# Attention in 128-query chunks: scores kept in SBUF pages, maxima sent through DRAM

## The chip, the cores and the metric

The kernel runs on one core of one Trainium2 chip. The metric is the device time of one execution in microseconds (us); the time before is 3614.04 us, the median of three runs (3613.12 to 3618.05). Engines are named as the profile names them: PE is TensorE, DVE is VectorE, ACT is ScalarE, POOL is GpSimd, and SP issues nearly all DMAs.

## The reference, cut to what matters

The kernel computes one transformer block on x of 8 batches, 1024 tokens and 512 channels, in f32. A condition gives shifts, scales and gates.

```
mod = silu(condition) @ Wada + bada                       # 6 parts: sh_a, sc_a, gt_a, sh_m, sc_m, gt_m
xm = layernorm(x, g1, be1) * (1 + sc_a) + sh_a
q, k, v = heads(xm @ Wqkv)                                # 16 heads of 32 channels
scores = q @ k.T * 32 ** -0.5                             # causal mask: -inf above the diagonal
x = x + gt_a * (softmax(scores) @ v @ Wproj + bproj)
xm = layernorm(x, g2, be2) * (1 + sc_m) + sh_m
x = x + gt_m * (gelu(xm @ W1 + b1) @ W2 + b2)
```

The softmax subtracts each query's maximum. Only the attention between q, k, v and the projection `Wproj` changes here.

## The kernel before, in words

The work is cut into 16 blocks of 512 tokens (`blocks`): an even block is the first half of a batch and attends to itself alone, an odd block is the second half and attends to both halves. A block has four groups of four heads (128 channels, `NC` = 4, `HPG` = 4); a head's 32 channels fill one quarter of PE's rows, so the four heads' score matmuls run side by side.

**The linear work** (q, k, v, the two layers of the MLP) is written as Strassen products: `matmul` at L201 issues four matmuls of 128 rows by 32 columns, weights come through a ring of nine 256 KB pieces (`RING`, `fetch`, L335 and L337 on SP). Results leave three PSUM banks (`banks`) on DVE or ACT (`copy_out`, `combine_out` at L193). An f32 matmul of the program shows as two instructions in the trace.

**Attention of one group** makes the scores twice. `scores_at_once` (L1389) puts queries on partitions and keys along the free dimension, 512 columns at a time for four heads, in the PSUM tile `st` (four banks, one buffer). DVE adds the causal mask on the diagonal (L1403) and reduces the maxima (L1406). `split_maxima` (L1420 to L1428) splits each maximum into three bf16 numbers, `maxima_rows` turns them into rows by bf16 matmuls (L1444), and ACT copies them out (L1450). `weights_T` then makes the scores again with keys on partitions (L1469), and bf16 matmuls subtract the maxima inside PSUM (L1481). ACT takes the exponential from PSUM into one of three `pT` tiles (L1493), POOL zeroes what lies above the diagonal (L1498), `weigh` multiplies by v (L1521), and `add_weights` sums the weights of all keys on POOL (L1594). `finish` sums them over partitions with a matmul by ones (L1539), ACT copies the sums and the result out (L1545, L1548), DVE inverts in four parts (L1554), and POOL multiplies (L1571).

**The order** is fixed when the kernel is built. A planner keeps a clock for each engine (`now`), notes each instruction's cost and when its results are due, and interleaves the attention units with the linear steps listed in `plan`: `step_aside` issues linear work while a unit is not ready, and `pace` spreads a window's linear work over its attention units. Each engine, and SP's queue, executes its list in that order and waits on semaphores.

Of the kernel before, what the change touches and what calls it, by code (L numbers as in the profile page):

```python
# [9 lines left out]
F32 = mybir.dt.float32  # L10
BF16 = mybir.dt.bfloat16
# [11 lines left out]
def kernel(  # L23
# [48 lines left out]
    RING = 9  # L72

# [153 lines left out]
    def mlp_steps(n):  # L227
# [7 lines left out]
        + [("mod", 3), ("at", 2), ("v", 1), ("mod", 4), ("columns_m",), ("k", 2), ("gates", "m")],  # L235
    }
    late = []
    for w in range(1, NB):
# [7 lines left out]
        if w == NB - 1:  # L246
            steps = late[:1] + [("load_xr", n)] + rows_a + [("proj", n), ("mt", n)] + late[1:]
            steps += [("v", w)] + rows_m + own + m[3:6]
            late = m[6:]
        else:  # L250

            steps = late + [("v", w), ("load_xr", n)] + rows_a + [("proj", n), ("k", w + 1)]
            if w == 1:
                steps = [("load_xr", n)] + rows_a + [("proj", n)]
            steps += [("mt", n), ("q", w + 1)] + rows_m + own
# [10 lines left out]
    plan[NB] = [("load_xr", n), late[0], ("beside", late[1]), ("proj", n), ("mt", n)] + mlp_steps(n)  # L266
# [120 lines left out]
    mask = const.tile([P, 2 * P], F32, tag="mask", name="mask")  # L387
    for i in range(2):
        make_causal_mask(nc, mask[:, ts(i, P)], MASKED)
# [4 lines left out]
    minus_ones = const.tile([P, P], BF16, tag="minus_ones", name="minus_ones")  # L394
    nc.gpsimd.memset(minus_ones, -1.0)
    mcols = const.tile([P, NTT, P], BF16, tag="mcols", name="mcols")
    nc.gpsimd.memset(mcols, 0.0)
    ident_b = const.tile([P, P], BF16, tag="ident_b", name="ident_b")
    nc.vector.tensor_copy(ident_b, ident)


    cond_act = tmp.tile([P, TB], F32, tag="top", name="cond_act", bufs=1)[:B, :]
# [41 lines left out]
    def norm_columns(name, shift_at, gain_at, o_g, o_b):  # L444
# [3 lines left out]
        one_plus = small.tile([P, NC, B], F32, tag="onep", name=f"onep{name}")  # L448
# [165 lines left out]
    def modulated(key, gain, shift, b, guards):  # L614
# [19 lines left out]
        for c in range(NC):  # L634
# [22 lines left out]
            if c == 1:  # L657
                nc.vector.tensor_tensor(part["T1"], part["T1"], part["B11"], ALU.subtract)
                note("DVE", 700, [at["B11"], at["T1"]], [at["T1"]], port=True)
        nc.vector.tensor_tensor(part["T2"], part["B22"], part["T1"], ALU.subtract)  # L660
# [14 lines left out]
    qTs, kTs, vs = {}, {}, {}  # L675
    projected, valued = set(), set()
# [163 lines left out]
    def project_T(step, store, pool, tag, done):  # L840

        n = step[1]
        dst = pool.tile([P, NC, TB], F32, tag=tag, name=f"{tag}_{n}")
        store[n] = dst
# [405 lines left out]
    def step_aside(reads, writes):  # L1250


        while threads():
            if linear_wait() == NEVER:
                hurry()
# [512 lines left out]
```

## Time and profile before

| What | Value |
|---|---|
| Median of three runs | 3614.04 us |
| Span of the profiled execution | 3610.1 us |
| The profiled execution's own time, taken as span plus the 3.9 us between span and median | 3614.0 us |
| PE, DVE, ACT, POOL busy | 98%, 58%, 37%, 56% of the span |
| Granted TensorE clock, mean | 0.995 |
| DMA engines' share | 38.8% on the main queue, 430.35 MB |

The profile shows one execution, which has no time of its own beside its span; the runs around it lie 3.0 to 8.0 us above that span. A line of a group reads: code line, engine, operation, output and inputs, shape, count, then busy time and the mean duration of one instruction. Busy time is the union of the group's intervals, so a mean duration holds the pipeline's latency too; the distance between two starts in the timeline is what a stretch of matmuls costs in a row.

### The profile page before, as it was taken

What the parts mean: (1) busy time and instruction counts of PE and PEld (TensorE: products, weight loads), DVE (VectorE), ACT (ScalarE), POOL (GpSimd) and SP (SyncE); (2) the same over time, 40 slices, a digit from 0 to 9 for tenths busy, and PEclk for the clock granted to TensorE, in tenths of its full rate; (3) what the DMA queues carried; (4) which work ended last, traced back from release to release, by engine and by line L of the source; (5) the groups of instructions that cost most, each with busy time, mean ns of one, the idle gap of its engine ahead of it and who ended that gap; (6) DMA issues with size and microseconds to landing.
All of it is one profiled execution on the core that took longest, in us unless ns stands there. A gap on an engine that the chain in (4) does not pass through costs nothing.

```text
span 3610.1 us, 121129 instructions
## 1 busy us (share of the span) xinstructions
PE 3537.6 (98%) x54821; PEld 1777.0 (49%) x54821; DVE 2078.8 (58%) x2316; ACT 1325.9 (37%) x1388; POOL 2038.3 (56%) x2187
## 2 busy tenths in 40 slices
PE   8999999999999999999999999999999999999999
PEld 5434445445554455544555455454554545545445
DVE  6765675563755547465464655746557455564663
ACT  2335334252433523335243351424524244232421
POOL 3666746665456753666536665456654566544660
PEclk9989999999999999999999999999999999999999
DMA  6633333434343343433434334343343433435334
GB/s 202 220 117 104 109 104 110 127 98 128 112 118 110 104 133 113 133 92 98 133 109 148 91 93 132 105 141 101 99 128 105 139 101 101 124 92 155 90 111 138
DMA packets 307894, 430.35 MB, mean 119 GB/s; under 512 B 25900, under 2 KB 176236, under 8 KB 307380
## 3 DMA queue, kind: packets, MB, share of 16 engines
q1 hardware_dynamic: 307264, 422.56, 38.8%
q8 instruction: 432, 7.08, 0.8%
q14 instruction: 82, 0.67, 0.1%
q10 hardware_dynamic: 116, 0.03, 0.0%
HBM read 394.12 MB, written 28.38 MB: 117 GB/s over the span
## 4 chain that ended last, share of the span: by engine, by line
PE 90%; DVE 4%; POOL 2%; ACT 2%; issue 1%; DMA 0%; SPq 0%; ACTq 0%; DVEq 0%; POOLq 0%
PE bank L201 62%; PE st L1469 8%; PE sc L1389 8%; PE po L1521 7%; DVE mx L1406 2%; PE st L1481 2%; PE bank L641 2%; PE bank L1539 2%; POOL pT L1594 1%; POOL xr L161 1%; ACT pT L1493 1%; DVE hT L1003 0%; PE bank L1444 0%; DVE xr L158 0%; ACT hT L945 0%
## 5 line engine op out<-in xcount | busy, mean ns | idle before, releaser
L1594 POOL TENSOR_TENSOR pT<-pT,pT 128x384 f32<-128x384 f32 (+2 forms) x1266 | 1195.6, 981 | 400.4 <-PE po L1521 211.0
L1493 ACT ACTIVATE pT<-st 128x2048 f32<-128x2048 f32 x288 | 541.0, 1878 | 858.2 <-PE st L1481 826.5
L201 PE MATMUL bank<-w,hT 128*32 128x256 f32 x14336 | 805.6, 381 | 1.0 <-ACT rec L1545 0.9
L1406 DVE TENSOR_REDUCE mx<-sc 128x4 f32<-128x2048 f32 (+3 forms) x380 | 658.5, 1754 | 147.7 <-PE sc L1389 140.6
L201 PEld LDWEIGHTS bank<-w,hT 128*32 128x32 f32 x14336 | 455.2, 110 | 338.4 <-issue 42.7
L201 PE MATMUL bank<-xm_m,w 128*32 128x256 f32 x8192 | 498.3, 381 | 3.1 <-ACT xm_m L651 3.0
L201 PE MATMUL bank<-t_m,w 128*32 128x256 f32 x6144 | 392.2, 381 | 0.4 <-DVE t_m L660 0.4
L1498 POOL TENSOR_SCALAR_AFFINE_SELECT pT<-pT 128x512 f32<-128x512 f32 x256 | 162.1, 651 | 400.4 <-ACT pT L1493 400.4
L201 PEld LDWEIGHTS bank<-xm_m,w 128*32 128x32 f32 x8192 | 254.9, 110 | 229.9 <-issue 62.5
L1389 PE MATMUL sc<-kT,qT 32*128 32x512 f32 (+3 forms) x3040 | 331.6, 524 | 7.6 <-DVE mx L1406 7.0
L1469 PE MATMUL st<-qT,kT 32*128 32x512 f32 (+3 forms) x3072 | 330.9, 523 | 6.7 <-DVE mx L1406 5.0
L1403 DVE TENSOR_TENSOR sc<-sc,mask 128x1024 f32<-128x1024 f32 (+1 forms) x159 | 161.5, 1016 | 278.9 <-PE sc L1389 238.9
L1521 PE MATMUL po<-pT,v 128*32 128x512 f32 (+3 forms) x3072 | 305.8, 493 | 10.2 <-POOL pT L1498 10.2
L201 PEld LDWEIGHTS bank<-t_m,w 128*32 128x32 f32 x6144 | 187.1, 110 | 197.2 <-issue 81.7
L201 PE MATMUL bank<-xm_a,w 128*32 128x256 f32 x3968 | 239.8, 380 | 0.0
L201 PE MATMUL bank<-w,qT 128*32 128x512 f32 x2048 | 237.8, 595 | 0.0
L1554 DVE RECIPROCAL rec<-rec 128x128 f32<-128x128 f32 x256 | 226.0, 919 | 6.0 <-ACT rec L1545 6.0
L1389 PEld LDWEIGHTS sc<-kT,qT 32*128 32x128 f32 x3040 | 130.8, 184 | 175.7 <-ACT pT L1493 81.3
L1469 PEld LDWEIGHTS st<-qT,kT 32*128 32x128 f32 x3072 | 130.1, 184 | 164.4 <-issue 71.6
L1493 ACT ACT_TABLE_LOAD x88 | 112.9, 1283 | 205.8 <-PE st L1481 205.3
L201 PE MATMUL bank<-t_a,w 128*32 128x256 f32 x2944 | 188.5, 380 | 0.0
L193 DVE TENSOR_TENSOR hT<-bank,u_u 128x512 f32<-128x512 f32 x192 | 128.4, 683 | 97.0 <-PE bank L201 96.2
(207 smaller groups left out, 3521.3 us busy)
## 6 DMA issues: line engine op xcount, KB each, us to landing
w<-in_L_cond_W_dram SPq DMA_DIRECT2D x384, 256.0 KB
w<-kept_up_S SPq DMA_DIRECT2D x256, 256.0 KB
w<-kept_down_S SPq DMA_DIRECT2D x256, 256.0 KB
w<-kept_qkv_S SPq DMA_DIRECT2D x180, 256.0 KB
w<-in_L_cond_Wqkv_dram SPq DMA_DIRECT2D x147, 256.0 KB
hat<-in_x_dram SPq DMA_DIRECT2D x64, 256.0 KB
w<-in_L_cond_Wproj_dram SPq DMA_DIRECT2D x64, 256.0 KB
xr<-in_x_dram SPq DMA_DIRECT2D x64, 256.0 KB
```

The source lines that it names most:

```text
L193: nc.vector.tensor_tensor(out, src, other, op)
L201: nc.tensor.matmul(ps[r, :], lhsT[:, r], rhs, start=start, stop=stop, skip_group_check=True)
L641: nc.tensor.transpose(banks[bank][:, ts(t, P)], got[t][:, ts(c, P)], ident)
L1389: nc.tensor.matmul(sc[:, j, c0 : c0 + w], qTs[n][r, gg, ts(qt, P)], keys_of(n, kh)[r, gg, :w], start=True, stop=True, skip_group_check=True,)
L1403: nc.vector.tensor_tensor(place, place, shape_of.to_broadcast(place.shape), ALU.add)
L1406: nc.vector.tensor_reduce(maxima[n, gg][:, kh, qt, :], sc[:, :, c0 : c0 + w], axis=AX.X, op=ALU.max)
L1469: nc.tensor.matmul(st[:, j, c0 : c0 + w], kT[r, gg, ts(k % NTT, P)], qT[r, gg, TB - w :], start=(c0 == 0), stop=False, skip_group_check=True,)
L1493: nc.scalar.activation(pT[:, :, :used], st[:, :, :used], AF.Exp, scale=scale)
L1498: nc.gpsimd.affine_select(diagonal, diagonal, pattern=[[0, HPG], [1, P]], compare_op=ALU.is_ge, fill=0.0, base=0, channel_multiplier=-1,)
L1521: nc.tensor.matmul(po[r, TB - w :], v[:, k % NTT, g * P + j * hd : g * P + (j + 1) * hd], pT[:, j, c0 : c0 + w], start=(k == 0), stop=last ...
L1554: nc.vector.reciprocal(some, some)
L1594: nc.gpsimd.tensor_tensor(into, into, pT[:, j, c0 : c0 + w], ALU.add)
```

## The change

Scores are made once, with keys on partitions, and attention goes in chunks of 128 queries (four to a group, 256 in all). A chunk's scores are made tile by tile, 128 keys by 128 queries for four heads. In a chunk of an odd block there are five to eight such tiles, in two units; in one of an even block one to four, in one unit. Over all chunks there are 1152 tiles in 384 units.

DVE adds the mask in PSUM to the diagonal tile, ACT copies the masked scores into SBUF `pages` (16 pages of one tile each), and DVE takes the maximum over the tiles, first by a reduction and for the second unit by one operation for each tile. Four PE transposes and a reduction on DVE give the maxima with queries on partitions; SP writes these 128 by 4 numbers to DRAM, waits for them to land, and reads them back broadcast to 128 partitions (`mb`, two buffers). DVE or POOL subtracts `mb` in the pages, ACT takes the exponential in place, PE multiplies by v, and POOL (or DVE) adds the tiles up. The ones matmul, the copy of the sums and the inversion are done for each chunk, and DVE reads the result in PSUM for the quotient.

Gone are the first pass of scores, the bf16 splits and rows, the subtraction on PE, POOL's zeroing of the diagonal and the copy of the result from PSUM. Keys lie in four half tiles instead of three whole ones; the residual of the last block goes into four pages; `attend` becomes a loop that picks among transposes, sums, linear work, values and scores by their planned waits. The diff, cut to its core (removed lines are those printed above):

```diff
+    PAGES = 16
+    ROWS = 2
...
-    plan[NB] = [("load_xr", n), late[0], ("beside", late[1]), ("proj", n), ("mt", n)] + mlp_steps(n)
+    plan[NB] = [late[0], ("beside", late[1]), ("load_xr", n), ("proj", n), ("mt", n)] + mlp_steps(n)
...
+    key_halves = [kvp.tile([P, 2, TB], F32, tag=f"kT{i}", name=f"kT_{i}", bufs=1) for i in range(4)]
...
-        yield [("attended", n)], []
+        yield [("attended", n), "hats"], []
...
+    def units_of(n, c):
+        count = NTT * blocks[n][1] + c + 1
+        parts = -(-count // NTT)
+        sizes = [count // parts + (i < count % parts) for i in range(parts)]
+        return [list(range(sum(sizes[:i]), sum(sizes[: i + 1]))) for i in range(parts)]
...
+    pages = pp.tile([P, PAGES, HPG, P], F32, tag="pages", name="pages")
...
+    def scores():
...
+        st = ps_st.tile([P, HPG, TB], F32, tag="st", name=f"st_{ci}_{u}")
+        for i, kt in enumerate(kts):
+            kT = kTs[n - h + kt // NTT][g // 2]
             for j in range(HPG):
                 r = slice(j * hd, (j + 1) * hd)
                 nc.tensor.matmul(
+                    st[:, j, ts(i, P)],
+                    kT[r, g % 2, ts(kt % NTT, P)],
+                    qTs[n][r, g, ts(c, P)],
...
+        if last:
+            diagonal = st[:, :, ts(len(kts) - 1, P)]
+            nc.vector.tensor_tensor(
+                diagonal, diagonal, mask.unsqueeze(1).to_broadcast([P, HPG, P]), ALU.add
+            )
...
+        for i, page, count in runs_of(some):
+            nc.scalar.copy(
+                pages[:, page : page + count].rearrange("p k j q -> p j k q"),
+                st[:, :, i * P : (i + count) * P].rearrange("p j (k q) -> p j k q", q=P),
+            )
...
             nc.vector.tensor_reduce(
+                maxima[ci],
+                st[:, :, : len(kts) * P].rearrange("p j (k q) -> p j q k", q=P),
+                axis=AX.X,
+                op=ALU.max,
             )
...
+        else:
+            for i in range(len(kts)):
+                nc.vector.tensor_tensor(maxima[ci], st[:, :, ts(i, P)], maxima[ci], ALU.max)
...
+    def transpose_maxima():
...
+        for j in range(HPG):
+            nc.tensor.transpose(banks[bank][:, ts(j, P)], source[:, j, :], ident)
...
+        nc.vector.tensor_reduce(
+            m, banks[bank].rearrange("p (j k) -> p j k", k=P), axis=AX.X, op=ALU.max
+        )
...
+    def run_sends():
+        for ci in list(m_cols):
+            if due([("m", ci)]) > now["PE"]:
+                break
+            at = kept.tile([HPG, P], F32, tag=f"kept_m_{ci}", name=f"kept_m_{ci}")
+            nc.sync.dma_start(at.rearrange("j q -> q j"), m_cols.pop(ci))
+            m_sent[ci] = at
+            written["m sent", ci] = now["PE"] + 2500
+        for ci in list(m_sent):
+            if due([("m sent", ci)]) > now["PE"] or (ci >= ROWS and ci - ROWS not in released):
+                break
...
+            row = rowp.tile([P, HPG * P], F32, tag="mb", name=f"mb_{ci}", bufs=ROWS)
+            at = m_sent.pop(ci)
+            nc.sync.dma_start(row, at.rearrange("j q -> (j q)").unsqueeze(0).to_broadcast([P, HPG * P]))
+            written["mb", ci] = now["PE"] + 3500
...
+            if max(now["DVE"], t) + wide + margin[0] < max(now["POOL"], t) + 1290 * count:
+                place = pages[:, page : page + count].rearrange("p k j q -> p k (j q)")
+                nc.vector.tensor_tensor(
+                    place, place, row.unsqueeze(1).to_broadcast(place.shape), ALU.subtract
+                )
...
+                for i in range(page, page + count):
+                    place = pages[:, i].rearrange("p j q -> p (j q)")
+                    nc.gpsimd.tensor_tensor(place, place, row, ALU.subtract)
...
+            nc.scalar.activation(place, place, AF.Exp, scale=scale)
...
+                either(total, flat[0], flat[1], ALU.add, page_keys(some[:2]), [key])
...
+                either(total, total, flat[i], ALU.add, [key, ("pg", some[i])], [key])
...
                     v[:, kt % NTT, g * P + j * hd : g * P + (j + 1) * hd],
-                    pT[:, j, c0 : c0 + w],
+                    pages[:, page, j, :],
...
+            nc.tensor.matmul(banks[bank][r, :P], ones[:, :hd], total[:, j, :], start=True, stop=True)
...
+                nc.vector.tensor_tensor(qTs[n][:, g, :], outs.pop((n, g)), rec, ALU.mult)
...
+            options = [
+                (transpose_wait(), 0, transpose_maxima),
+                (finish_wait(), 1, finish),
+                (value_wait(), 2, values),
+                (score_wait(), 3, scores),
+            ]
+            linear = linear_wait()
+            pick = next((o for o in options[:2] if o[0] <= 50), None)
+            if pick is None and done_linear[0] < stream["due"] and linear <= 100:
+                pick = (linear, 4, work)
```

In the built order of the changed kernel DVE does 270 of the subtractions (740 tiles) and POOL the other 412 tiles one by one; POOL does 878 of the 896 additions.

## The prediction

> **What bounds the kernel now.** I read busy time and the chain first, then stretches, then shapes, then the timeline.
>
> ```profile
> PE 3537.6 (98%) x54821; PEld 1777.0 (49%) x54821; DVE 2078.8 (58%) x2316; ACT 1325.9 (37%) x1388; POOL 2038.3 (56%) x2187
> PE 90%; DVE 4%; POOL 2%; ACT 2%; issue 1%; DMA 0%; SPq 0%; ACTq 0%; DVEq 0%; POOLq 0%
> ...
> 20.00:196.00 176.00, 158.97 (x2554) 85.62 (x2552) 133.11 (x168) 48.66 (x56) 88.81 (x114) 0.96 0.65 214
> 430.00:590.00 160.00, 158.57 (x2444) 77.79 (x2438) 103.82 (x116) 63.13 (x71) 76.71 (x97) 1.00 0.37 113
> 1923.00:2164.00 241.00, 238.60 (x3680) 119.01 (x3680) 129.24 (x143) 93.39 (x93) 155.61 (x165) 1.00 0.38 112
> 2164.00:2358.00 194.00, 192.44 (x3012) 98.02 (x3008) 120.14 (x133) 66.80 (x74) 97.84 (x111) 1.00 0.40 118
> ```
>
> PE bounds every stretch. The columns of the stretches are window, length, and busy time of PE, its weight loads, DVE, ACT, POOL. An odd block (third line) uses 54% of DVE, the even one after it 62%. Only the first stretch, with DVE at 76%, leaves PE idle for 10%.
>
> ```profile
> L1389 PE MATMUL sc<-kT,qT 32*128 32x512 f32 (+3 forms) x3040 | 331.6, 524 | 7.6 <-DVE mx L1406 7.0
> ...
> 906.17 1.15 PE L1469 MATMUL st<-qT,kT 32*128 32x384 f32 x16
> 907.14 0.40 PE L1481 MATMUL st<-mrow,minus_ones 32*128 32x384 bf16 x8
> 907.47 0.41 PE L1444 MATMUL bank<-ident_b,mcols 128*32 128x128 bf16 x16
> 907.71 1.46 PE L1521 MATMUL po<-pT,v 128*32 128x512 f32 x16
> ...
> 1004.34 0.31 PEld L1469 LDWEIGHTS st<-qT,kT 32*128 32x128 f32 x8 [0.41 <-DVE mv_a L556]
> 1004.35 1.14 PE L1469 MATMUL st<-qT,kT 32*128 32x512 f32 x8
> 1005.31 0.39 PE L1481 MATMUL st<-mrow,minus_ones 32*128 32x512 bf16 x4
> ...
> 616.66 2.18 PE L641 MATMUL bank<-ident,hat 128*128 128x128 f32 x16
> 618.86 20.93 PE L201 MATMUL bank<-w,hT 128*32 128x256 f32 x384
> ...
> L1003 DVE TENSOR_TENSOR hT<-hT x32: 1212/2293/2312, 346.5 to 3559.5; 128x1024 f32<-128x1024 f32 x32
> ...
> 3607.01 0.33 SPq L1060 DMA_DIRECT2D out_dram<-xr  x1
> ...
> 4.71 3.96 SPq L335 DMA_DIRECT2D w<-in_L_cond_Wada_dram  x8
> 8.65 0.40 PE L201 MATMUL bank<-condT,w 128*32 128x8 f32 x16 [1.38 <-DMA w<-in_L_cond_Wada_dram]
> ...
> SPq L337 <- PE bank L201: 1626.1, 638, 19.8
> ```
>
> From start to start, 512 score columns for four heads take 0.96 us (1004.35 to 1005.31), the row subtraction 0.33 (907.14 to 907.47), one L1444 set 0.24, a transpose 0.14 (16 in 2.20).
>
> **PE, removed.** The chain gives L1389 8.0% of 3610, 289 us. The subtraction: 288 units (the count of exponentials) by 0.325, 94 us. L1444: 64 by 0.24, 15 us. Together 398 us.
>
> **PE, added.** Transposes: 256 chunks by 4 by 0.147 us (L641's busy time, 75.1 us over 512), 151 us. Score visits rise from 288 (L1469) to 384; one costs some 0.1 us more than its columns on entry and 0.1 on leaving, so 96 by 0.2 is 19 us. The columns of scores (1152 tiles of 128), values and ones sums are those of before. Narrower pieces: a visit with 384 and 128 columns took 0.97 us, one with 512 took 0.96, hence 0.01 us for a tile, 12 us. From below that is zero. From above it is the loads: eight took 0.31 us, a tile's eight matmuls at column rate 0.24, so 0.07 by 1152, 81 us. I take 12, since the 128-column piece is in that visit itself.
>
> The Trainium skill, "TensorE: Matmul & The Clock Gate", section "Back-to-back issue gap", speaks against it: a load and its matmul sustain about 81 ns at 128 columns against 131 ns at 512, 2.5 times as much for a column. By that rule, as an estimate, scores (276 us) and values (251 us) would grow by some 775 us and the kernel would take about 4,300 us. No run here shows these two figures, and 0.97 beside 0.96 disagrees with them for these quarter tiles.
>
> Net: -398 + 151 + 19 + 12 = -216, a span of 3394 us (3382 to 3463 with the bounds) if all else hides as now.
>
> **DVE.** Removed: reductions 664, masks 161, splits and sums 28, together 853 us. Added, by rows of the same size (0.69 us for 512 elements, 2.29 for 2048, so 0.14 plus 0.54 for a tile): masks 256 by 0.69, 178; first-unit reductions 224 over 736 tiles, 427; second-unit maxima 384 by 0.69, 265; reductions after the transposes 256 by 0.68, 174; quotients 63 by 0.69, 43; subtractions 270 over 740 tiles, 443. That is 1530, and DVE comes to 2756 us, 78% of a span of 3530. The last price is a lower bound: L1003 shows one operation on two SBUF tensors at 1212 ns or at 2293, while POOL works; half a us for each of 270 makes 135 more. I take 60.
>
> The Trainium skill, "SBUF — State Buffer", section "SBUF: two separate sides", says a DVE operation with two SBUF inputs and a POOL operation that reads SBUF hold one port pair in turn, each for its whole length. L1003's two durations agree. As an estimate by that rule, POOL's 215 us and DVE's 66 us of such work in the odd block below exclude each other, 281 us, as long as PE needs there, and POOL loses cover too.
>
> **POOL** sheds 1196 + 162 + 69 + 80 and takes up 412 + 878 tiles by 1.28 us, 1651: near 2180 us. **ACT** sheds 653 (exponentials, three copies) and adds 1152 tiles twice by 0.43 with 454 instructions by 0.17 each way, and 256 copies by 0.28: near 1885 us, 53%.
>
> **Where it concentrates.** In the built order, between the last quotients of blocks 6 and 7 (an odd block), I count instructions by these rows: PE 262 us and some 20 of form switches, DVE 232 (up to 259 with the port), POOL 215, ACT 180. The even blocks beside it have PE 105 to 123, DVE 96 to 103. The order thus puts more linear work beside odd blocks than now, but DVE stands at 82 to 92% of PE there against 54%, and the three banks that PE needs empty through DVE, behind 2.3 us reductions and subtractions. Idle PE therefore grows. Lower bound: today's 72 us. Upper bound: the 20 to 196 us stretch, 10% idle at 76% DVE. I take 6%, as part of that stretch's idle time is the start: 3322 busy us / 0.94 = 3534. With 10 us for the longer way out of the last chunk, 3544.
>
> **The DMA round trip.** Each chunk adds a 128 by 4 write and a 256 KB broadcast; SP's 512 issues by 0.33 to 0.46 us (some 200 us) fit into the 1626 us that it waits for PE ahead of L337 alone. SP then waits for its own write to land, and weight loads queue behind it. Nine pieces at 1.72 us of PE (32 instructions, 1000.78 to 1002.50 in the timeline) are 15 us of cover. DVE's subtraction waits for the broadcast; evacuations queue behind it, and PE behind them. For chunk 118 the order leaves 5.4 us of PE work from write to first subtraction. The last store ends at most 3.1 us after its issue (3607.01 to 3610.1), and PE first used a weight 3.9 us after its issue (4.71 to 8.65, with a wait for it shown): 7.0 at most, against 3.8 if both take only 1.9, the last store's 0.33 of issue and the 1.6 that SP then waits for it. So between 1.6 us late and 1.6 early; I take neither, the middle.
>
> Quotients on DVE instead of POOL are counted; moved residual loads and the "hats" guard I cost at nothing, hidden by the linear work; without that cover a load costs some 4 us a block.
>
> **Forecast.** The profiled execution's own time is 3610.1 + 3.9 = 3614.0, which is the median. 3544 + 3.9 = 3548 us, its own range 3440 to 3606.
>
> **Rivals.**
> A, all hides: 3394 + 4 = 3398. For it, PE at 98% now, and linear work to fill; against it, DVE's 82 to 92%.
> B, slower: the broadcast comes late, and DVE stands with PE's evacuations behind it. It decides from 0.26 us a chunk (66 / 256); at 0.6 us it gives 3700. For it, 7.0 against 5.4; against it, two rows of 256 KB where the write is 2 KB.
> C, slower: DVE and POOL become the bound beside odd blocks, PE idle for 10%: 3322 / 0.90 + 4 = 3695. For it, the first stretch; against it, 99% PE at 65% DVE.
>
> **How the numbers follow.** 0.2% is about what a measurement tells from no change. Forecast 0.44 (0.04 of it within 0.2%), A 0.15, B 0.22, C 0.19. Faster 0.55, same 0.04, slower 0.41. The range 3400 to 3760 leaves half of A below and 0.12 of B and C above.
>
> **What would show it.** Right: L1389 and L1481 gone from the chain, PE's L1340 near 0.24 us a tile, transposes near 0.15, DVE near 78%, PE near 94%. Wrong: L1340 above 0.3 us a tile (the loads bind), idle DVE before L1463 ended by a DMA (B), PE waiting for DVE at L202 by over 250 us (C).

## The result, and the profile after

The changed kernel takes 6298.98 us, the median of four runs (6289.64 to 6321.89), against 3616.05 us for the kernel before on the same chip: 1.743 times as long, with an interval of 1.739 to 1.747. The forecast was 3548 us, and its range ended at 3760. The profiled execution has a span of 6294.6 us.

First the page's busy times, clock and DMA packets.

```profile
PE 3982.8 (63%) x64037; PEld 2358.9 (37%) x64037; DVE 2846.8 (45%) x3212; ACT 1792.3 (28%) x1991; POOL 2395.8 (38%) x1668
...
PEclk8768788787887888878788797787878877778788
...
DMA packets 480017, 499.36 MB, mean 79 GB/s; under 512 B 165164, under 2 KB 315500, under 8 KB 479412
```

PE's busy time has risen from 3537.6 to 3982.8 us although it has less to do, and it is busy for 63% of the span, not 98%. DVE stands at 45%, ACT at 28%, POOL at 38%: no engine is full. The mean granted clock is 0.807, where it was 0.995. Below 512 bytes there are 165,164 packets.

Then the costliest groups of the page: after the bar come busy time, the mean of one in ns, and the idle time of the engine just before them with what ended most of it.

```profile
L1470 POOL TENSOR_TENSOR pages<-pages,mb 128x512 f32<-128x512 f32 x412 | 669.4, 1650 | 1942.7 <-DMA mb<-kept_m 1920.9
...
L1463 DVE TENSOR_TENSOR pages<-pages,mb 128x1536 f32<-128x1536 f32 (+3 forms) x270 | 537.8, 2012 | 1037.9 <-DMA mb<-kept_m 1024.2
...
L1553 PE MATMUL po<-pages,v 128*32 128x128 f32 x9216 | 430.0, 337 | 584.6 <-ACT pages L1478 533.0
```

POOL and DVE stand idle for 1,921 and 1,024 us until a broadcast row `mb` has come. This is the sign that the prediction named for rival B. Its sign for C, PE waiting at L202 for DVE by over 250 us, is there too: these waits add up to 461 us. In the run below that has neither the DMA nor the wait behind the copy (e5) they are 54, so this sign alone does not tell C from B. Its sign for binding weight loads was badly set: L1340's 442.3 us are 0.38 for each of 1152 tiles, above the 0.3 named, but the same measure gives L1469 of the kernel before 0.29 (330.9 us).

The waits, summed: who waited, on which line, for what, us in total, times, longest. First SP's queue, then the engines.

```profile
SPq L1435 <- DMA kept_m<-m: 1958.5, 242, 12.1
```

```profile
POOL pages L1470 <- DMA mb<-kept_m: 1920.9, 142, 42.7
ACT pages L1478 <- POOL pages L1470: 1340.9, 157, 20.8
DVE pages L1463 <- DMA mb<-kept_m: 1024.2, 160, 19.6
...
DVE max L1369 <- ACT pages L1358: 752.6, 208, 17.0
...
PE po L1553 <- ACT pages L1478: 533.0, 105, 23.0
...
DVE max L1378 <- ACT pages L1358: 350.6, 126, 14.1
...
PE bank L1408 <- DVE max L1378: 224.2, 64, 19.5
```

This is a chain. SP waits 242 times, 8.1 us each, for its own write of the maxima to land; POOL and DVE wait for the broadcast that SP issues after that; ACT's exponentials wait for the subtraction; PE's values wait for the exponentials. It is not the only way to PE: of PE's idle time its waits view puts 1,322 us down to DVE, 711 to ACT and 145 to POOL. DVE works through its list in order and stands 1,024 us for broadcasts and 753 + 351 us behind ACT's copies; behind it wait PE's transposes (521 us) and the emptying of PE's banks (L202, 461 us).

One piece of the timeline (start in us, duration, engine, instruction; in brackets the idle time before it and what ended it) shows two chunks.

```profile
3015.71 1.87 ACT L1358 COPY pages<-st 128x2048 f32<-128x2048 f32 x1 [1.18 <-DVE st L1352]
...
3017.61 2.29 DVE L1369 TENSOR_REDUCE max<-st 128x512 f32<-128x2048 f32 x1 [1.99 <-ACT pages L1358]
...
3019.09 0.33 SPq L1435 DMA_DIRECT2D mb<-kept_m  x1
...
3019.95 0.46 SPq L1425 DMA_DIRECT2D kept_m<-m  x1
...
3024.08 2.52 POOL L1470 TENSOR_TENSOR pages<-pages,mb 128x512 f32<-128x512 f32 x2 [10.22 <-DMA mb<-kept_m]
...
3031.45 0.34 SPq L1435 DMA_DIRECT2D mb<-kept_m  x1
...
3036.56 3.70 POOL L1470 TENSOR_TENSOR pages<-pages,mb 128x512 f32<-128x512 f32 x3 [7.51 <-DMA mb<-kept_m]
```

The write of 3019.95 is followed by its broadcast at 3031.45, 11.5 us later, and POOL subtracts at 3036.56, another 5.1 us later. Over all 256 chunks the broadcast's issue comes 10.45 us after the write's in the median (8.4 to 17.3). The prediction had put the whole trip, write and broadcast, at 3.8 to 7.0 us. The first two lines show a second thing, which it had not seen at all: ACT copies the score banks from 3015.71 to 3017.58, and DVE's reduction over the same banks begins at 3017.61, when the copy is over.

### The profile page after: what moved, and what is told of

Read it like the earlier page. It is cut to its first block, busy times and chain, and to the rows that moved or that the text cites. A ratio compares the mean times of both kernels' runs of the same rounds, so it can differ in the third digit from the quotient of the medians.

```text
span 6294.6 us, 142245 instructions
## 1 busy us (share of the span) xinstructions
PE 3982.8 (63%) x64037; PEld 2358.9 (37%) x64037; DVE 2846.8 (45%) x3212; ACT 1792.3 (28%) x1991; POOL 2395.8 (38%) x1668
## 2 busy tenths in 40 slices
DMA packets 480017, 499.36 MB, mean 79 GB/s; under 512 B 165164, under 2 KB 315500, under 8 KB 479412
## 5 line engine op out<-in xcount | busy, mean ns | idle before, releaser
L1470 POOL TENSOR_TENSOR pages<-pages,mb 128x512 f32<-128x512 f32 x412 | 669.4, 1650 | 1942.7 <-DMA mb<-kept_m 1920.9
L1478 ACT ACTIVATE pages<-pages 128x1536 f32<-128x1536 f32 (+3 forms) x454 | 573.8, 1283 | 2251.3 <-POOL pages L1470 1340.9
L1463 DVE TENSOR_TENSOR pages<-pages,mb 128x1536 f32<-128x1536 f32 (+3 forms) x270 | 537.8, 2012 | 1037.9 <-DMA mb<-kept_m 1024.2
L202 PE MATMUL bank<-w,hT 128*32 128x256 f32 x14336 | 901.6, 407 | 138.8 <-ACT hT L954 58.4
L162 POOL TENSOR_TENSOR sum<-sum,pages 128x512 f32<-128x512 f32 x668 | 898.9, 1346 | 173.0 <-ACT pages L1478 111.1
L1358 ACT COPY pages<-st 128x1536 f32<-128x1536 f32 (+3 forms) x454 | 555.3, 1239 | 1026.9 <-DVE st L1352 655.7
L1553 PE MATMUL po<-pages,v 128*32 128x128 f32 x9216 | 430.0, 337 | 584.6 <-ACT pages L1478 533.0
L1369 DVE TENSOR_REDUCE max<-st 128x512 f32<-128x1536 f32 (+2 forms) x224 | 427.8, 1910 | 775.5 <-ACT pages L1358 752.6
L202 PEld LDWEIGHTS bank<-w,hT 128*32 128x32 f32 x14336 | 483.6, 118 | 507.0 <-issue 142.0
L162 POOL TENSOR_TENSOR sum<-pages 128x512 f32<-128x512 f32 x210 | 277.5, 1321 | 1023.4 <-ACT pages L1478 524.0
L202 PE MATMUL bank<-xm_m,w 128*32 128x256 f32 x8192 | 561.9, 411 | 141.4 <-DVE u_u L194 78.2
L1553 PEld LDWEIGHTS po<-pages,v 128*32 128x32 f32 x9216 | 322.4, 135 | 703.5 <-ACT pages L1478 587.2
L1340 PE MATMUL st<-qT,kT 32*128 32x128 f32 x9216 | 442.3, 329 | 165.7 <-DVE max L1369 123.3
L202 PE MATMUL bank<-t_m,w 128*32 128x256 f32 x6144 | 421.7, 407 | 120.2 <-DVE hT L194 76.2
L1340 PEld LDWEIGHTS st<-qT,kT 32*128 32x128 f32 x9216 | 358.7, 222 | 313.1 <-DVE max L1369 159.8
L202 PEld LDWEIGHTS bank<-xm_m,w 128*32 128x32 f32 x8192 | 277.7, 118 | 346.5 <-DVE u_u L194 84.7
L202 PE MATMUL bank<-xm_a,w 128*32 128x256 f32 x3968 | 289.8, 429 | 69.3 <-DVE p_q L186 25.1
L202 PE MATMUL bank<-t_a,w 128*32 128x256 f32 x2944 | 229.8, 443 | 140.3 <-DVE m L1412 48.1
L202 PEld LDWEIGHTS bank<-t_m,w 128*32 128x32 f32 x6144 | 204.6, 117 | 281.6 <-DVE hT L194 81.2
```

The costliest lines, as they stand in the source:

```text
L162: nc.gpsimd.tensor_tensor(out, a, b, op)
L202: nc.tensor.matmul(ps[r, :], lhsT[:, r], rhs, start=start, stop=stop, skip_group_check=True)
L1340: nc.tensor.matmul(st[:, j, ts(i, P)], kT[r, g % 2, ts(kt % NTT, P)], qTs[n][r, g, ts(c, P)], start=True, stop=True, skip_group_check=True,)
L1358: nc.scalar.copy(pages[:, page : page + count].rearrange("p k j q -> p j k q"), st[:, :, i * P : (i + count) * P].rearrange("p j (k q) -> ...
L1369: nc.vector.tensor_reduce(maxima[ci], st[:, :, : len(kts) * P].rearrange("p j (k q) -> p j q k", q=P), axis=AX.X, op=ALU.max,)
L1463: nc.vector.tensor_tensor(place, place, row.unsqueeze(1).to_broadcast(place.shape), ALU.subtract)
```

## The experiments

Theory 1 says that the write's landing sets the pace, in the form 1a because of its 512 single numbers; theory 2 blames the broadcast as well; theory 3 and C say that DVE and POOL hold each other up; theory P says that the order was written with too short times; S that two engines do not read one score bank side by side; D that the depth of the pages is too small; M that it is the making of the maxima.

In e1 and e2 DVE, ACT and POOL execute the same instructions in the same order as in the changed kernel. For every other run the planner wrote a new order, so what such a run gains or loses holds its order too. Runs with the row by PE, and those with four rows of 512 bytes, keep the mask in bf16; the latter also keep the tile of ones in 32 columns instead of 128.

| Run | What differs | Median, us | To before (95%) | PE busy / idle, us | Clock |
|---|---|---|---|---|---|
| before | | 3616 | 1 | 3538 / 73 | 0.995 |
| after | the change | 6299 | 1.743 (1.739 to 1.747) | 3983 / 2312 | 0.807 |
| e1 | no write, a fixed row broadcast | 4901 | 1.356 (1.353 to 1.358) | 3672 / 1229 | 0.882 |
| e2 | 128 runs of 16 bytes | 5329 | 1.474 (1.471 to 1.477) | 3773 / 1556 | 0.860 |
| e3 | order with 10.5 and 5 us | 5556 | 1.537 (1.532 to 1.541) | 3888 / 1677 | 0.840 |
| e12 | 12 pages | 6380 | 1.765 (1.759 to 1.771) | 4022 / 2349 | 0.795 |
| e11 | 4 rows of 512 bytes | 5103 | 1.411 (1.407 to 1.416) | 3802 / 1298 | 0.868 |
| e4 | row by PE, no DRAM | 5012 | 1.387 (1.384 to 1.389) | 3832 / 1173 | 0.881 |
| e6 | e4, order knows the copy's wait | 4801 | 1.328 (1.326 to 1.331) | 3778 / 1019 | 0.885 |
| e5 | e4, maxima before the copy | 4527 | 1.253 (1.251 to 1.255) | 3724 / 788 | 0.911 |
| e16 | e5, order with longer prices | 4571 | 1.264 (1.262 to 1.266) | 3727 / 838 | 0.906 |
| e7 | after, maxima before the copy | 5919 | 1.638 (1.634 to 1.642) | 3971 / 1953 | 0.820 |
| e15 | e11, e7 and order with 3.5 and 5 us | 4754 | 1.314 (1.312 to 1.316) | 3769 / 989 | 0.884 |
| e9 | e5 without subtractions | 4240 | 1.173 (1.170 to 1.176) | 3659 / 583 | 0.921 |
| e10 | no maxima, ones subtracted | 3782 | 1.046 (1.043 to 1.049) | 3325 / 455 | 0.933 |
| e13 | transposes and rows alone | 3910 | 1.081 (1.079 to 1.083) | 3545 / 361 | 0.956 |
| e14 | reductions alone | 3740 | 1.034 (1.032 to 1.036) | 3314 / 424 | 0.934 |
| e8 | no maxima at all | 3486 | 0.964 (0.962 to 0.967) | 3248 / 239 | 0.965 |

Busy time and clock are from each run's profiled execution; idle is its span less the busy time.

### Is it the write?

**e1, a fixed row.**

```diff
+    fixed = kept.tile([HPG, P], F32, tag="kept_fixed", name="kept_fixed")
+    nc.sync.dma_start(fixed, ones[:HPG, :])
...
-            at = kept.tile([HPG, P], F32, tag=f"kept_m_{ci}", name=f"kept_m_{ci}")
-            nc.sync.dma_start(at.rearrange("j q -> q j"), m_cols.pop(ci))
+            at = fixed
+            m_cols.pop(ci)
```

> Left out: the maxima are still made but not written; every chunk broadcasts one row of ones that was written to DRAM at the start, so the subtraction takes 1 from every score instead of the query's maximum. The 256 broadcasts, their issues on SP and the subtractions stay; the 256 writes and the wait for their landing go. Theory 1 (the write's landing, 10.4 us from issue to the broadcast's issue, sets the pace; the rest of the round trip is hidden as predicted): 3,500 to 3,900 us. Theory 2 (the broadcast's own 5 us and its 256 KB are as much to blame): 4,300 to 5,500 us. Theory 3 (DVE and POOL hold each other up at the subtractions, the DMA is a symptom): over 5,500 us.

Measured 4,901 us. The write and the wait for it are worth 1,398 us, about half of the loss. It fell into theory 2's range, but not for its reason: of PE's 1,229 idle us its waits view puts 809 down to DVE and 1 to a DMA. DVE waits for a broadcast only for 103 us before its subtractions (1,024 in the changed kernel). POOL still waits 670 us for one, but PE's waits for POOL come to 159.

**e2 and e11, the same 2 KB in fewer pieces.**

```diff
 # e2                                       # the subtraction then reads the row with a step of four
-            nc.sync.dma_start(at.rearrange("j q -> q j"), m_cols.pop(ci))
+            nc.sync.dma_start(at, m_cols.pop(ci))          # at is 128 queries by 4 heads
...
 # e11
...
+            nc.tensor.transpose(banks[bank][:HPG, :P], m, ident)
...
+            nc.scalar.copy(turned, banks[bank][:HPG, :P])
...
+            nc.sync.dma_start(at, turned)                  # 4 heads by 128 queries
```

> The same numbers are written as 128 runs of 16 bytes (query by head) instead of 512 single numbers, and the subtraction reads the row with a stride of four. Theory 1a (the landing's time goes with the number of pieces written): the write lands in 3 to 4.5 us instead of 10.4 and the time falls to 3,700 to 4,700 us. Theory 1b (any write to DRAM that is read back takes 10 us, however many pieces): the gap between the two issues on SP stays over 9 us and the time stays within 5% of 6,299 us. Theory 3 (DVE and POOL): no change or slower, as the strided row can only lengthen the subtraction.

> The changed kernel, but the 128 by 4 maxima are first turned by one transpose on TensorE and a copy of 4 by 128 on ScalarE, so that the write is four rows of 512 bytes; row, broadcast and subtractions are as they were. Theory 1a (the landing goes with the number of pieces): from issue to the broadcast's issue 2 to 3.3 us, and 4,950 to 5,200 us in all, near the 4,901 us of the kernel with a fixed row. If waiting for one's own write in SP's queue costs much in itself: over 5,400 us.

From the write's issue to the broadcast's, the median over the 256 chunks is 10.45 us with 512 single numbers, 3.31 us with 128 runs of 16 bytes and 1.31 us with four rows. The timeline of e11 shows two of them.

```profile
2518.55 0.27 SPq L1436 DMA_DIRECT2D kept_m<-turned  x1
...
2519.77 0.32 SPq L1446 DMA_DIRECT2D mb<-kept_m  x1
...
2524.57 0.27 SPq L1436 DMA_DIRECT2D kept_m<-turned  x1
...
2525.74 0.33 SPq L1446 DMA_DIRECT2D mb<-kept_m  x1
```

This distance holds whatever SP had to do between the two. In the chunks in which it issued nothing between them (79, 79 and 99) the medians are 9.29, 1.96 and 1.23 us. What SP stood for its own writes, summed as above, falls from the 1,958.5 us of the changed kernel to (e2, then e11)

```profile
SPq L1435 <- DMA kept_m<-m: 257.8, 161, 4.5
```

```profile
SPq L1446 <- DMA kept_m<-turned: 153.6, 151, 4.1
```

The bytes are the same in all three. Theory 1a holds, 1b falls. e11 lies in the range that 1a gave it; the other form of the write is worth 6,299 - 5,103 = 1,196 us, 4.7 us for each of 256 chunks, net of the transpose and the copy that it needs. e2 missed its range by some 630 us, though its landing came as expected. Its subtraction reads the row with a step of four, which raised DVE's subtractions from 538 to 854 us and POOL's from 669 to 831. That is the smaller part of the miss: e11 reads the row as before and takes 5,103, and e1 has no write at all and takes 4,901. The range left out the other losses that are found below.

**e3 and e12, a better order and less depth.**

```diff
 # e3
-            written["m sent", ci] = now["PE"] + 2500
+            written["m sent", ci] = now["PE"] + 10500
-            written["mb", ci] = now["PE"] + 3500
+            written["mb", ci] = now["PE"] + 5000
 # e12
-    PAGES = 16
+    PAGES = 12
```

> The order written out with the times as measured: 10.5 us for the write (was 2.5) and 5 us for the broadcast (was 3.5). Nothing else changes. Theory P (the order is wrong because it was made with too short times; there is enough other work to put between): 3,600 to 4,500 us. Theory 1 with a limit on depth (16 pages and two rows hold two to three chunks, and SP issues in order, so that the time cannot be hidden whatever the order): over 5,000 us.

> The changed kernel with 12 pages in place of 16. Theory D (the round trip cannot be covered because the pages hold only two to three chunks between scores and values): a quarter less depth costs 6 to 25%, 6,700 to 7,900 us. If the depth of pages is not what holds it: within 3% of 6,299 us.

e3 took 5,556 us: an order that knows the times saves 743 us, but does not hide the trip, since POOL and DVE still wait 681 and 396 us for broadcasts. In 125 of its 256 trips another write is issued before the broadcast (13 in the changed kernel), and the median from write to broadcast rises to 14.3 us. SP stands only 321 us for its own writes there, so much of that distance is other work in its list. e12 took 6,380 us, 1.3% more for a quarter of the pages: in the changed kernel theory D falls. e3 lies in the range of the theory that the depth limits it, but this is no proof of it: e1, with no write to wait for, takes 4,901, so most of what keeps e3 above 5,000 us is something else. The rows (two), SP's order, and other depths under e3's order were not varied.

### What is left without DRAM

**e4, the row made by TensorE.** The maxima are reduced to bf16; four matmuls with a maximum as weights for all 128 rows and the identity moving lay it out over all partitions, and ACT copies the bank to the row.

```diff
+            nc.tensor.matmul(
+                banks[bank][:, ts(j, P)], m[:, j : j + 1].to_broadcast([P, P]), ident_b, start=True, stop=True,
+                skip_group_check=True,
+            )
...
+        nc.scalar.copy(row, banks[bank])
```

> No DRAM round trip: the maxima are rounded to bf16, TensorE lays each query's maximum out over all partitions with four bf16 matmuls of 128 columns (the maxima as weights, the identity moving) and ScalarE copies the bank into the row; what is subtracted is the same for all keys of a query. The subtractions in the pages stay as they are. PE adds 256 times 4 by 0.06 to 0.15 us, 60 to 150 us, ScalarE 256 by 0.55, 140 us. Theories 1 and 2 (the DMA): the predicted 3,548 us and these, 3,600 to 3,800 us. Theory 3 (DVE and POOL): over 4,500 us.

Measured 5,012 us, where theories 1 and 2 said 3,600 to 3,800. Theory 3 had named over 4,500, and the number lies there; e9 and e10 below price what it blames, the subtractions, at under 300 us. With no round trip at all the kernel is still 39% slower than before. So the DMA was the largest single cause and not the only one. Its waits:

```profile
DVE max L1371 <- ACT pages L1360: 524.2, 217, 10.5
...
DVE max L1380 <- ACT pages L1360: 369.4, 128, 11.5
...
PE bank L1410 <- DVE max L1380: 179.9, 63, 10.2
```

DVE stands for 524 + 369 us until ACT's copy of the score banks is over, and PE behind DVE. In the timeline:

```profile
3006.55 0.70 DVE L1354 TENSOR_TENSOR st<-st,mask 128x512 f32<-128x512 f32 x1 [0.64 <-PE st L1342]
...
3007.36 1.86 ACT L1360 COPY pages<-st 128x2048 f32<-128x2048 f32 x1 [0.78 <-DVE st L1354]
...
3009.26 2.29 DVE L1371 TENSOR_REDUCE max<-st 128x512 f32<-128x2048 f32 x1 [2.01 <-ACT pages L1360]
...
3011.60 0.42 PEld L1410 LDWEIGHTS bank<-ident,max 128*128 128x128 f32 x4 [1.55 <-DVE max L1371]
```

The mask ends at 3007.25, the copy runs until 3009.22, the maximum until 3011.55, and then the transposes can start. The chain from scores to maximum holds the copy, which it does not need.

**e5, e6 and e7, who reads first.** e5 takes the maxima before the copy, on top of e4, and tells the order's planner that the copy waits for them; e7 does the same alone in the changed kernel. e6 leaves the copy first and only tells the planner that the maximum waits for it.

```diff
 # e5, e7: the block that takes the maxima stands before this one
-            note_act(170 + 428 * count, None, reads, page_keys(range(page, page + count)))
+            note_act(170 + 428 * count, None, [*reads, key], page_keys(range(page, page + count)))
...
 # e6
-            note("DVE", 170 + 530 * len(kts), reads, [key])
+            note("DVE", 170 + 530 * len(kts), [*reads, *page_keys(some)], [key])
...
```

> The row by TensorE, as in the run of 5,012 us, and the maxima taken from the score banks before ScalarE copies these banks to the pages, not after. Theory S (two engines do not read one score bank side by side: DVE stands 524 + 369 = 893 us behind ScalarE's copies there, and PE behind DVE): ScalarE stands instead, which has 62% of its time free, and the time falls by 700 to 1,200 us, to 3,800 to 4,300. Theory D (the long chain from scores over maximum, row, subtraction and exponential to values, with 16 pages, sets the pace, whoever reads first): within 4% of 5,012 us.

> The row by TensorE, the copy first as in the run of 5,012 us, but the order is written with the maximum starting when the copy has ended, as the profile shows it. Theory S with lost engine time (DVE stands idle during the copy, whatever the order): 4,700 to 5,012 us. Theory P (the loss comes from an order that takes the two for parallel): below 4,300 us.

> The changed kernel with its round trip through DRAM, and only the maxima taken before the copies. If the losses of the round trip and of the serial reading add up (6,299 to 5,012 and the gain of the run beside this): 5,200 to 5,600 us. If the round trip hides the other loss: over 6,000 us.

e5 took 4,527 us, 485 less than e4, and now ACT does the waiting:

```profile
ACT pages L1376 <- DVE max L1362: 579.4, 168, 11.3
ACT pages L1376 <- DVE max L1371: 432.3, 101, 11.2
```

ACT waits longer (1,012 us) than DVE did (893), and PE's idle time still falls from 1,173 to 788 us. S holds in its mechanism; the gain is below the 700 us that it had named. e6 took 4,801 us, in the range named for lost engine time; P, in the form below 4,300, falls. To know the wait is worth 211 us. e5's 485 us hold such knowledge too; against e6, which has it, the turn of the readers is worth 274. In the changed kernel (e7) both together are worth 380 us, between the two expectations: a fifth less than without the round trip.

**e16, longer prices in the order**, on top of e5: 1.53 us for POOL's subtraction, 0.76 us a page for DVE's, longer sums, 0.4 us for a change of form on PE.

```diff
-    SYNC, PIPE, SWITCH, TABLE = 100, 250, 150, 1283
+    SYNC, PIPE, SWITCH, TABLE = 150, 350, 400, 1283
...
-                    note("POOL", 1290, [("mb", ci), ("pg", i)], [("pg", i)])
+                    note("POOL", 1530, [("mb", ci), ("pg", i)], [("pg", i)])
```

> The kernel of 4,527 us (row by TensorE, maxima first) with its order written by longer prices, nearer to the trace: 1.53 us for POOL's subtraction (was 1.29), 0.76 us a page for DVE's (0.54), sums at 1.4 us (1.29), 0.4 us for a change of form on PE (0.15) and 0.1 us more for a result to be seen. Theory P (what is left is an order made with too short times): 4,000 to 4,300 us. If it is work that does not fit beside PE in whatever order: within 3% of 4,527 us.

Measured 4,571 us, 1% more. With these prices the order loses; theory P, in this form, does not explain what is left. Other prices or another rule for picking were not tried.

**e8 to e10, e13 and e14: leaving out.**

```diff
 # e9, from e5                        # e8 leaves out the maxima, their transposes and rows as well
-                nc.vector.tensor_tensor(
-                    place, place, row.unsqueeze(1).to_broadcast(place.shape), ALU.subtract
-                )
...
-                    nc.gpsimd.tensor_tensor(place, place, row, ALU.subtract)
 # e10, from e8, with the subtractions
+    one_row = rowp.tile([P, HPG * P], F32, tag="mb", name="one_row")
 # e13, from e9
-            nc.vector.tensor_reduce(
-                maxima[ci],
...
+            maxima[ci] = pages[:, some[0]]
```

> Left out: reductions to maxima, their transposes, the write, the broadcast and the subtractions; the exponential is taken of the scaled score itself. Scores made once, copied to pages, exponentials, sums and values stay. PE has 3,394 - 151 = 3,243 us of work by the prediction's prices. If all that lost the time is in what is left out: 3,300 to 3,600 us. If the pages, the copies to them or POOL's sums hold PE up by themselves: over 3,800 us.

> Left out of the kernel that took 4,527 us (row by TensorE, maxima first): the subtractions in the pages. Maxima, transposes and rows are still made, and the order still holds each exponential until its row is due, but nothing is subtracted. Theory C (the subtractions on DVE and POOL, 523 and 748 us, and their standing in each other's way): below 3,950 us. Theory M (making the maxima: 867 us of reductions on DVE, 128 and 200 us of PE waiting on them and on sums): over 4,250 us.

> The kernel without maxima (3,486 us) and the subtractions put back, of a row of ones that lies in SBUF from the start. Left out are thus the maxima, their transposes and rows. Theory C: 3,800 to 4,200 us, the subtraction alone lengthens it. Theory M: 3,486 to 3,650 us. If neither run moves far, it takes the two together: the subtractions cost little unless they have to wait for a row.

> The kernel without subtractions (4,240 us), and also without the reductions over the score banks: what is transposed is the first page of each chunk as copied. Left out are thus the true maxima and the subtraction; transposes, the small reduction after them and the row by TensorE stay. If the 754 us between 3,486 and 4,240 are the price of PE's own added visits (1,024 transposes, 1,024 bf16 matmuls, some 300 us of PE in that run): 4,000 to 4,250 us. If they are the reductions of 693 us on DVE between the scores and the copy: 3,750 us or less.

> The kernel without maxima (3,486 us) with the reductions over the score banks put back, ahead of the copies; their results are used by nothing. Left out: transposes, rows, subtractions. If DVE's reductions hold the copies and so PE: 3,800 us or more. If PE's own visits are the price: 3,490 to 3,650 us.

e8 took 3,486 us, 3.6% less than before, and PE's line of its page is

```profile
PE 3248.2 (93%) x63013; PEld 2022.0 (58%) x63013; DVE 1546.5 (44%) x2132; ACT 1768.7 (51%) x1822; POOL 1716.9 (49%) x1259
```

The 3,394 - 151 = 3,243 us of the expectation is a span that still holds the 72 us in which PE stood idle before. As busy time the prediction's price for this work is 3,322 - 151 = 3,171 us; measured are 3,248, 77 more. With the prediction's own 6% of idle PE and its 14 us at the end, the same sum gives an estimate of 3,387 us for this kernel, and it took 3% more, with PE idle for 7%. Scores made once, the pages, the copies to them, the exponentials and sums thus do nearly what the prediction expected of them. Everything beyond 3,486 us comes with the maxima:

| | no subtraction | with subtraction |
|---|---|---|
| no maxima | 3,486 (e8) | 3,782 (e10) |
| maxima, rows by PE | 4,240 (e9) | 4,527 (e5) |

The subtractions cost 296 us without and 287 us with the maxima, so the two nearly add up, and it makes little odds whether the row has been there from the start. None of e9, e10, e13 and e14 lies in a range named for it: each lies between its rivals. C and M both have a part. The 754 us of the maxima split into 254 us for the reductions alone (e14) and 424 us for transposes and rows alone (e13); the remaining 76 us come only with both. The groups of PE's matmuls in e13:

```profile
L1397 PE MATMUL bank<-ident,pages 128*128 128x128 f32 x1024 | 172.6, 292 | 13.0 <-ACT rec L1565 4.2 <-ACT pages L1360 3.7 <-ACT mb L1425 2.6
...
L1419 PE MATMUL bank<-ident_b,m 128*128 128x128 bf16 x1024 | 103.4, 224 | 17.0 <-DVE m L1401 16.8
```

Transposes (predicted 151 us) and the rows that stand in for the DMA are 276 us of PE there; PE's idle time grew by 122. In e14 PE's work hardly grows (66 us) and its idle time grows by 185.

**e15, three mends together** in the kernel that keeps the round trip: four rows of 512 bytes, maxima first, 3.5 and 5 us in the order.

```diff
-            written["m sent", ci] = now["PE"] + 2500
+            written["m sent", ci] = now["PE"] + 3500
...
```

> The changed kernel with its round trip, mended in three places at once: the write in four rows of 512 bytes, the maxima taken before the copies, and the order written with 3.5 us for the write and 5 us for the broadcast. If the gains seen one by one add up (6,299 - 1,196 - 380 or more): 4,500 to 4,800 us, near the 4,527 us of the kernel with rows by TensorE, and still slower than before. If the broadcast keeps a price of its own: 4,800 to 5,200 us.

Measured 4,754 us, in the range for gains that add up. Those of e11 (1,196) and e7 (380) would give 4,723 by themselves, so the third mend, the times in the order, added nothing to them that shows; with the long write (e3) it had been worth 743. It is still 31% slower than before. No version that subtracts the maxima came near the kernel before; e8 beats it, but without a maximum its exponentials are safe only while scores are small, so it is a bound here and no replacement.

The loss, then, in a row of runs that each differ from the last by one step and by the order written for it: 6,299 to 5,103 by the write's pieces (1,196), to 5,012 by leaving DRAM, net of PE's own rows (91), to 4,527 by the order of readers and the planner's knowledge of it (485), to 4,240 without subtractions (287), to 3,486 without maxima and the transposes and rows that they need (754).

## Why the prediction was wrong

**PE's work: nearly right, 77 us short.** Without the transposes 3,171 us were predicted, and e8 shows 3,248: of 367 us to be saved against 3,538, 289 are there. The groups of scores, values and ones sums, first before, then in e8:

```profile
L1469 PE MATMUL st<-qT,kT 32*128 32x512 f32 (+3 forms) x3072 | 330.9, 523 | 6.7 <-DVE mx L1406 5.0 <-ACT pT L1493 0.7
L1521 PE MATMUL po<-pT,v 128*32 128x512 f32 (+3 forms) x3072 | 305.8, 493 | 10.2 <-POOL pT L1498 10.2
...
L1539 PE MATMUL bank<-pT,ones 128*32 128x512 f32 x512 | 68.0, 593 | 1.2 <-DVE xm_m L645 1.2
```

```profile
L1340 PE MATMUL st<-qT,kT 32*128 32x128 f32 x9216 | 389.0, 301 | 57.4 <-ACT pages L1358 53.1 <-issue 4.1
...
L1516 PE MATMUL po<-pages,v 128*32 128x128 f32 x9216 | 347.1, 289 | 18.5 <-ACT pages L1441 16.2 <-issue 1.5 <-DVE qT L1566 0.4
...
L1547 PE MATMUL bank<-sum,ones 128*32 128x128 f32 x1792 | 100.4, 299 | 126.5 <-POOL sum L162 125.4 <-DVE hT L194 0.5
...
L1547 PE MATMUL bank<-pages,ones 128*32 128x128 f32 x256 | 12.8, 273 | 0.3 <-DVE qT L186 0.3
```

The narrow matmuls cost more than the 12 us taken. Scores grew by 58 us, for 12 and 19 for the visits predicted and 100 with the upper bound; values and ones sums, costed at nothing, by 41 and 45. The linear work's records, of the same count, grew by 12. Records of neighbouring groups overlap, so PE's total, 77 us, is the better measure of all such errors together. The 775 us that the prediction derived, as an estimate, from the Trainium skill, "TensorE: Matmul & The Clock Gate", section "Back-to-back issue gap", are not there. It was right not to take them.

**The DMA round trip: the step with the largest loss.** "So between 1.6 us late and 1.6 early; I take neither" rested on two rows of 256 KB. The prediction saw that the write is only 2 KB and took that as a reason for less. What counts here is the pieces: 512, each 4 bytes, and 10.45 us from the write's issue to that of the broadcast that waits for it, where 1.9 to 3.1 had been taken. Rival B named the mechanism, a late broadcast and DVE standing with PE's evacuations behind it, and the sign to look for, and gave it 0.22; but its price, 0.6 us a chunk, was an eighth of the 4.7 us that e11 measures for the write's form. The shape `j q -> q j` stood in the diff. The Trainium skill, "DMA: Bandwidth & Descriptors", section "Rules for kernel authors", says that a transfer whose last dimension is strided is lowered to one descriptor for each element and should be rearranged. The page counts agree: packets under 512 bytes are 165,164 in the changed kernel and 30,000 in e1, which has no write; of the 135,164 between them 256 by 512, 131,072, are the numbers, and some 16 more come with each write. What such a transfer takes no sentence there says; the runs give it.

**"Idle PE therefore grows ... I take 6%": failed too, with no DMA at all.** PE is idle for 23% of the span in e4 and 17% in e5. The sum had looked at how full DVE is (78% by the prediction; 2,847 us busy measured for 2,756 predicted, so this was near) and not at what each DVE instruction waits for. The step "first-unit reductions 224 over 736 tiles, 427" prices the reduction (428 measured) as if it ran beside ACT's copy. In the changed kernel 208 of the 224 wait for the copy to end, and what DVE has queued stands behind them. To let the maxima go first, with an order that knows it, was worth 485 us without the round trip and 380 with it. That the two share a tile could be read from the program. The Trainium skill, "PSUM — Partial Sum Buffer", section "PSUM bank collisions raise a hardware error", says that two engines must not touch one bank in the same partitions at once, two reads included. The runs agree with the waiting, 893 us of it in e4; what would happen without the wait, or with the two engines on different banks of the tile, was not tried. What reductions, transposes and rows still cost when the maxima go first is the 754 us between e8 and e9; the prediction had 151 us of transposes for it, and its 6% for all idle time together.

**The port on DVE and POOL: right in direction, small in size.** DVE's subtractions took 538 us (443 + 60 predicted). POOL's came to 1.65 us each in the mean, not 1.28; the median of all 412 is 1.27 and the longest 3.40, so a part of them is drawn out. The subtractions as a whole cost 287 to 296 us, and how much of this is the sharing was not measured by itself; the prediction, with DVE under PE, let them cost nothing beyond the 6%. Rival C's mechanism thus had its part, and at 3,695 us was priced too low as well.

**SP's queue: right in the main.** PE waits for a DMA for 6 us in all, so weight loads behind SP's 1,959 us of waiting were mostly covered by the ring, as the prediction said. For 121 us more of PE's idle time the profile names no releaser ("issue"); without the write (e1) that is 3 us. Whether these are late weights is not shown.

**The clock: a term that was missing.** The sum divided 3,322 us by 0.94 as though idle time had no price beyond itself. In the changed kernel the work priced at 3,322 us shows 3,983 us of busy time at a mean granted clock of 0.807. How much of the 661 us more is the clock is not separated (last section).

## What to carry to other kernels

Price a small DMA by the number of contiguous pieces that it writes, not by its bytes, and look for a transposed side in the access pattern: 512 numbers took 8 times as long as four rows of the same 2 KB. When an engine is to read a PSUM tile that another engine also reads, put the two durations one after the other and let the one on the critical chain go first. A sum of busy times bounds a kernel from below, and a span that already holds idle time is not such a sum. Before the sum is divided by a share of idle time, follow one unit through all its engines and write down what every instruction waits for.

## What the runs showed of the hardware that was not expected

The mean granted clock falls as PE's idle share rises, run by run with little scatter: 0.995 at 2% idle, 0.965 at 7%, 0.956 at 9%, 0.933 at 12%, 0.911 at 17%, 0.868 to 0.882 at 23 to 25%, 0.807 and 0.795 at 37%. The matmuls of the MLP's largest group, whose count is the same in all, take 805.6 us before, 799.5 in e8, 835 in e5 and 902 in the changed kernel, so down to a clock of 0.965 they did not grow at all. The Trainium skill, "TensorE: Matmul & The Clock Gate", section "What's actually happening", says that the clock is throttled unless the array has been busy of late; the order of the runs agrees. No run here sets the clock by itself, so how much of the growth is clock, and how much is that the matmuls come in shorter stretches, was not separated.

A write's landing grows with its pieces, though not by a fixed time each: where SP issued nothing between write and broadcast, the distance is 1.23, 1.96 and 9.29 us for 4, 128 and 512 pieces, 6 ns a piece between the first two and 19 between the last two. The trace's records of the single packets show only about 9 ns each.

A second operand read with a step of four numbers raised the shortest 512-element subtraction on DVE from 0.68 to 1.07 us, and on POOL from 1.25 to 1.51 us.
